# Issuing P's transpositions ahead of the output's product, and a group's sum of scales one stage after its squares

## The chip, the cores and the metric

The kernel runs on one core of one Trainium2 chip. A core has a matrix engine (TensorE, PE in the profile, with PEld for its loads of stationary operands), three engines for elementwise work (VectorE or DVE, ScalarE or ACT, GpSimd or POOL) and a sync engine (SyncE or SP), which here issues all transfers. Each engine takes its own list of instructions and waits on semaphores that the others raise. TensorE writes its results to PSUM, a small memory that VectorE and ScalarE read.

The metric is the device time of one execution in microseconds.

## The reference

Two batches of 512 tokens with 512 features go through one transformer layer in float32: causal attention with 32 query heads and 8 key and value heads of 128 features, the output product, a residual and a layer norm; then a feed-forward part, a residual and a layer norm.

```python
q = (hidden_states @ Wq)...; k = (hidden_states @ Wk)...; v = (hidden_states @ Wv)...
scores = einsum('bhqd,bhkd->bhqk', q, k) * HEAD_DIM ** -0.5     # causal
out = softmax(scores) @ v ; x = layernorm(x + out @ Wo)
base_out = x @ W_base.T + b_base
weights = sparsemax(x @ W_router.T + b_router)                  # 8 experts
expert_out = einsum(x @ lora_A, weights, lora_B)                # rank 16
x = layernorm(x + base_out + expert_out)
```

## The kernel before

**Groups, batches and steps.** A group is one key and value head with its four query heads. There are 8 groups and 2 batches, and each pair of a group and a batch is cut into 4 tiles of 128 query tokens. One such tile is a unit of work; the list `units` has 64 of them. The main loop runs over steps s = 0 to 59, and the last four units are worked off by `tail()`, which has an order written out by hand (`TAIL`). For most groups a batch's four steps are followed by the other batch's four, so a group takes eight steps. Within a pair, i = s mod 4 is the tile; this document calls its steps first, second, third and fourth. A causal tile i reads i + 1 blocks of keys, so later steps have more work.

**What a step issues.** The stages of a unit are spread over three steps:

- `unit_a` (this step's unit): four products of scores `s`, one for every 32 rows of the four heads together (L229, from the loop at L408); VectorE adds the mask and finds the maximum (L413), ScalarE takes the exponential with its row sums (L418); then `cut_p` writes P as a high and a low half in float16, the high half on ScalarE (L381), the low one on VectorE (L384), with the factors `ast` (L369, L371) between.
- `unit_t` (the previous step's unit): P, 6 to 30 blocks of 128 x 128 in the tile `phl`, is transposed by TensorE into PSUM tiles `px` (L340), eight blocks at a time, and ScalarE copies each eight to `pt` (L341). A copy of eight blocks is 1024 columns wide, the last of six is 768.
- `proj` (for the next pair): in the first step K and the first of Q's four products, in the second another of Q, in the third V, in the fourth the last two of Q. Each is 12 matmuls of 512 columns (V: 48 of 128), and its result is cut into halves by ScalarE and then VectorE (`cut_psum`, L233 and L234).
- `unit_c` (the unit of two steps ago): the output product `pw`, 12 matmuls of 512 columns, and a sum into `acc` on VectorE (L497).
- `unit_b` (the previous step's unit): P times V, `pv`, 6, 12, 18 or 24 matmuls, and its cut `o`.

The generator of `unit_t` is advanced by one group of eight blocks ahead of each projection, and what is left of it is issued later: before, right ahead of `unit_b` and after `unit_c`.

**PSUM buffers.** The tag `pj` has two buffers. The tiles `px`, the results of the projections (`pk`, `pq`, `pvp`), the sums `tot` and some of the feed-forward's tiles share them in turn. `S` has four (scores), `PV` and `wo` one each (`pv`, `pw`).

**Weights of a later group.** `prepare` loads a group's weights, finds their largest values (L123, VectorE), splits them into float16 halves on GpSimd (L117 to L120). Between stand the scales: `measure` takes the squares of the largest values on ScalarE (`sq`, L186), `total` adds them over the partitions with a product by ones on TensorE (`tot`, L128), and `scales` turns the sum into powers of two (L133 to L138, VectorE). This is done twice for a group: for Q, K and V in the four steps of a first batch, and for the output's rows in those of a second batch. `at(prepare(...), ...)` lists at which step each piece is issued, up to the generator's next `yield`; `advance` takes one piece after each projection and each `unit_b`, and the last call of a step takes all that are left.

**What sets the order.** The main loop's order in the source is a priority. The framework's scheduler places the instructions on each engine's list by this priority and by its own estimate of when operands and buffers are there. So the lists interleave the stages, and one moved line can move many instructions. The start (L777 on) and the tail are placed by hand.

Of the kernel before, what the change touches and what calls it, by code (L numbers as in the profile page):

```python
# [22 lines left out]
NG = 8  # L23
# [17 lines left out]
def kernel(  # L41
# [60 lines left out]
    def load_raw(src, name, rows=False):  # L102

        raw = sb.tile([P, 512], F32, tag="rawo" if rows else "raw", name=f"raw_{name}", bufs=4 if rows else 6)
        sync_load(raw, src if len(src.shape) == 2 else src.rearrange("p a c -> p (a c)"))
        return raw
# [6 lines left out]
    def split16(hi, lo, view, by, fast=False):  # L113

        if fast:
            first = nc.scalar.activation(hi, view, AF.Copy, scale=by)
        nc.gpsimd.tensor_scalar(view, view, by, 1.0, ALU.mult, ALU.mult)  # L117
        if not fast:
            first = nc.gpsimd.tensor_scalar(hi, view, 1.0, 1.0, ALU.mult, ALU.mult)
        return first.ins, nc.gpsimd.tensor_tensor(lo, view, hi, ALU.subtract).ins  # L120

    def amax(dst, view):
        nc.vector.tensor_reduce(dst, view, AX.X, ALU.max, apply_absolute_value=True)  # L123

    def total(sq, n, name, tag="pj"):

        tot = ps.tile([P, 8], F32, tag=tag, name=f"tot{name}", bufs=4 if tag == "S" else 2)
        nc.tensor.matmul(tot[:, :n], ones, sq[:, :n], start=True, stop=True)  # L128
        return tot

    def scales(sc, tot, n):

        nc.vector.tensor_scalar(  # L133
            tot[:, :n].bitcast(I32), tot[:, :n].bitcast(I32), 24, 23,
            ALU.logical_shift_right, ALU.logical_shift_left,
        )
        nc.vector.tensor_scalar(sc[:, 0, :n], tot[:, :n], 2.0**-109, 2.0 ** (64 - TOP), ALU.max, ALU.mult)
        nc.vector.reciprocal(sc[:, 1, :n], sc[:, 0, :n])  # L138
# [3 lines left out]
    def source(g, j):  # L142

        if j < 4:
            return wq[g * HPG + j]
        if j < 6:
            return (wk, wv)[j - 4][g]
        r0 = (g * HPG + j - 6) * P
        return wo[r0 : r0 + P, :]

    def w_tile(g, j):
        shape = [P, 2, KC, P] if j < 6 else [P, 2, HID]
        tag, bufs = ("w", 12) if j < 6 else ("wo", 8)
        W[(g, j)] = sb.tile(shape, F16, tag=tag, name=f"w{g}_{j}", bufs=bufs)
        return [W[(g, j)][:, q].rearrange("p a c -> p (a c)") if j < 6 else W[(g, j)][:, q] for q in range(2)]

    def prepare(g, js, raws=None):

        if raws is None:
            raws = [load_raw(source(g, j), f"{g}_{j}", j >= 6) for j in js]  # L160
            yield
        name = f"{g}_{js[0]}"
        rows = js[0] >= 6
        n = 1 if rows else 6
        if (g, rows) not in SC:
            yield from measure(g, js, raws, name, rows, n)
        sc = SC[(g, rows)]
        for k, (j, raw) in enumerate(zip(js, raws)):
            j = 0 if rows else j
            LAST[(g, js[k])] = split16(*w_tile(g, js[k]), raw, sc[:, 1, j : j + 1], g == 0)  # L170
            if k % 2:
                yield

    def measure(g, js, raws, name, rows, n):
        mx = sb.tile([P, 8], F32, tag="mx", name=f"mx{name}", bufs=2)
        for k, (j, raw) in enumerate(zip(js, raws)):
            j = k + 1 if rows else j
            with behind(mybir.EngineType.DVE) if g > 1 or rows else nullcontext():
                amax(mx[:, j : j + 1], raw)
            if k % 2:  # L180
                yield
        sc = sb.tile([P, 2, 8], F32, tag="sc", name=f"sc{name}", bufs=8)
        if rows:
            amax(mx[:, 0:1], mx[:, 1:5])
        sq = sb.tile([P, 8], F32, tag="sq", name=f"sq{name}", bufs=2)
        nc.scalar.activation(sq[:, :n], mx[:, :n], AF.Square)  # L186
        scales(sc, total(sq, n, name), n)
        SC[(g, rows)] = sc
        yield
# [153 lines left out]
    def proj(g, b, j):  # L343
        if j == 4:
            factors(g, b)
            end_k(g, b, mul_k(g, b))
        elif j == 5:
            end_v(g, b, mul_v(g, b))
            turn_v(g, b)
        else:  # L350
            end_q(g, b, j, mul_q(g, b, j))
# [79 lines left out]
    def unit_t(g, b, i, tag="pj"):  # L431

        phl = PH.pop((g, b, i))
        nb = 8 * i + 6
        PT[(g, b, i)] = pt = sb.tile([P, nb, P], F16, tag="PT", name=f"pt{g}_{b}_{i}", bufs=2)
        for k in range(0, nb, 8):
            n = min(nb, k + 8)
            turn_blocks(pt[:, k:n, :], phl[:, k * P : n * P], tag)
            yield
# [44 lines left out]
    def unit_c(g, b, i, first):  # L484
        o2 = OT.pop((g, b, i))
        if first:
            out_factor(g, b)
        pw = ps.tile([P, HID], F32, tag="wo", name=f"pw{g}_{b}_{i}", bufs=1)
        pairs = []
        for h in range(HPG):  # L490
            w2 = W[(g, 6 + h)]
            oh, ol = (o2[:, a, h].rearrange("p j q -> p (j q)") for a in range(2))
            pairs += [(oh, w2[:, 0, :]), (oh, w2[:, 1, :]), (ol, w2[:, 0, :])]
        mm3(pw, pairs)
        yield
        a = acc[b * NT + i]
        nc.vector.scalar_tensor_tensor(a, pw, LM[(g, b)][:, 7:8], a, ALU.mult, ALU.add)  # L497
        yield
# [94 lines left out]
    def behind(engine):  # L593

        return tc.issue_after(next(i for i in reversed(nc.cur_bb.bb.instructions) if i.engine == engine))
# [124 lines left out]
    def done(gen):  # L720
        for _ in gen:
            pass
# [3 lines left out]
    def step_ffn():  # L726
        for gen in list(live):
            if next(gen, "end") == "end":
                live.remove(gen)
# [7 lines left out]
    JS = (4, 0, 1, 5, 2, 3)  # L737
    ROWS = (6, 7, 8, 9)
# [38 lines left out]
    with tc.manual_schedule(engines={ET.PE, ET.DVE, ET.Activation, ET.Pool, ET.SP}):  # L777
# [10 lines left out]
        w1_raw = [load_raw(source(1, j), f"1_{j}") for j in JS[:2]]  # L788
# [81 lines left out]
    def step_live():  # L870
        step_ffn()
# [4 lines left out]
    def at(gen, *when):  # L876
        for u in when:
            plan[u].append(gen)
# [11 lines left out]
    def late_x(b, after):  # L890
        yield from behind_all(convert_x(b), *LAST[after])

    at(prepare(0, ROWS, wo_raw), 0, 0, 0)
    at(prepare(1, JS, w1_raw), 1, 1, 1, 2, 2, 2, 3, 3)
    at(prepare(1, ROWS), 4, 5, 5, 6, 6, 7, 7)
    at(late_x(1, (1, 3)), 5, 6, 7, 7)
    at(ffn_setup(), 20, 21, 21, 21, 21, 21, 28, 28, 29, 29, 36)
    for g in range(1, NG):
        u = NT * (starts[g] - 2) - (3 if g == NG - 2 else 0)
        if g > 1:  # L900
            at(prepare(g, JS), u - (1 if g == NG - 2 else 2), u, u, u + 1, u + 2, u + 2, u + 3, u + 3, u + 3)
        u += NT
        if g > 1:
            at(prepare(g, ROWS), u - 2, u, u + 1, u + 2, u + 2, u + 3, u + 3)

    def advance(last=False):
        while plan.get(s):
            next(plan[s].pop(0), None)
            if not last:
                break  # L910
# [44 lines left out]
    for s in range(len(units) - NT):  # L955
        if s < len(units):
            g, b, i = units[s]
            k = s // NT
            nx = groups[k + 1] if k + 1 < len(groups) else None
            done(unit_a(g, b, i))  # L960
            step_live()
            turns = unit_t(*units[s - LB]) if s >= LB else iter(())
            if nx:
                for j in ((4, 0), (1,), (5,), (2, 3))[i]:
                    next(turns, None)
                    proj(*nx, j)
                    advance()
            step_live()
        if s >= LC:
            n = s - LC  # L970
            u = units[n]
            done(unit_c(*u, n % NT == 0))
            step_live()
            if u[0] == NG - 1 and u[2] < NT - 1:
                live.append(ffn(u[2]))
        if s >= LB:
            done(turns)
            done(unit_b(*units[s - LB]))
            step_live()
            advance()  # L980
        advance(True)
# [58 lines left out]
```

## Time and profile before

| | us |
|---|---|
| Time, median of 3 (lowest, highest) | 780.69 (777.91, 781.45) |
| The profiled execution: its time | 780.98 |
| Its span in the profile | 779.2 |
| First, second, third, fourth step where nothing else falls in (s = 28, 29, 26, 27) | 11.70, 8.58, 8.55, 15.07 |
| Third and fourth step with the sum of an output group (s = 14, 15) | 9.46, 14.58 |
| ScalarE's copy of 1024 or 768 transposed columns, median of all | 1.00 |
| ScalarE's and VectorE's cut of a product of Q, median | 0.60, 0.69 |
| VectorE's sum of an output product into acc | 0.74 |

How it is read: a step's length is from the first scores product of one unit to that of the next. A row of the timeline gives the start, the length of the whole row, the engine, the line, the operation, the tiles written and read, and how many instructions it holds; in square brackets is the engine's idle time ahead of it and what ended it. The ends of matmuls are modelled and overlap the next start, so between rows of TensorE the difference of two starts tells more than start and end do. In the view of waits a row gives who waited for whom, the total, how often, and the longest.

### The profile page before, as it was taken

The page shows a single profiled execution, that of the slowest core. Times are in us where ns is not written, and L with a number is a line of the kernel's source. Part 1 is how long each engine was busy: PE and PEld are TensorE (multiplying, and loading weights), DVE is VectorE, ACT ScalarE, POOL GpSimd, SP SyncE. Part 2 cuts the span into 40 slices and gives each one's busy share as a digit, 9 for nine tenths or more (in the row PEclk, how much of TensorE's full clock was granted, in tenths as well). Part 3 has the DMA queues.
Part 4 walks back from the last instruction along what each step waited for, and adds up shares of the span by engine and source line. Part 5 has one row for each costly group of instructions (what it writes and reads, how often), then busy time and mean ns, then how long its engine had stood idle before and what let it go on. Part 6 is the DMA issues. An engine that isn't in the chain of part 4 may idle for free.

```text
span 779.2 us, 15455 instructions
## 1 busy us (share of the span) xinstructions
PE 739.1 (95%) x5630; PEld 465.6 (60%) x5630; DVE 528.4 (68%) x1701; ACT 512.2 (66%) x1294; POOL 314.3 (40%) x500
## 2 busy tenths in 40 slices
PE   9899999999998999999999999999999999998896
PEld 6666656555665755566565655666565656655653
DVE  6874866767584676748576675849576576865587
ACT  6797676767576676757577576757667676456630
POOL 5779350907036297633318067243615020200011
PEclk9899999999999999999999999999999999999999
DMA  8641110210102011110102012010000000000001
GB/s 314 213 136 41 43 55 2 55 28 29 28 2 69 2 42 56 28 55 1 55 3 82 1 55 82 2 55 1 1 1 2 2 1 1 15 14 14 1 7 64
DMA packets 17358, 32.22 MB, mean 41 GB/s; under 512 B 1920, under 2 KB 2176, under 8 KB 17280
## 3 DMA queue, kind: packets, MB, share of 16 engines
q1 hardware_dynamic: 17280, 31.22, 12.6%
q8 instruction: 44, 0.72, 0.4%
q14 instruction: 34, 0.28, 0.1%
HBM read 29.12 MB, written 2.10 MB: 40 GB/s over the span
## 4 chain that ended last, share of the span: by engine, by line
PE 35%; ACT 32%; DVE 18%; issue 5%; POOL 2%; DMA 0%; POOLq 0%; ACTq 0%; DVEq 0%
PE pq L229 11%; ACT s L418 10%; ACT pt L341 9%; ACT phl L381 8%; PE pw L229 7%; PE pv L229 7%; PE s L229 3%; DVE s L413 3%; PE px L340 3%; DVE mx L123 2%; ACT q L233 2%; DVE phl L384 2%; DVE q L234 2%; PE pa L229 2%; DVE o L234 1%
## 5 line engine op out<-in xcount | busy, mean ns | idle before, releaser
L229 PE MATMUL pw<-w,o 128*128 128x512 f16 x768 | 182.3, 380 | 0.0
L384 DVE SCALAR_TENSOR_TENSOR phl<-s,ast,phl 128x128 f16<-128x128 f32 (+7 forms) x352 | 128.7, 417 | 75.2 <-ACT phl L381 74.8
L341 ACT COPY pt<-px 128x1024 f16<-128x1024 f16 (+1 forms) x160 | 148.1, 937 | 44.0 <-PE px L340 43.6
L229 PE MATMUL pq<-xT,w 128*128 128x512 f16 x672 | 154.1, 379 | 7.6 <-DVE k L234 4.3
L413 DVE CUSTOM_DVE_ANT_0 s<-s,mask,lm 128x320 f32<-128x320 f32 (+15 forms) x256 | 118.9, 502 | 56.0 <-PE s L229 55.4
L418 ACT ACTIVATE s<-s,ast 128x320 f32<-128x320 f32 (+15 forms) x256 | 120.1, 471 | 33.8 <-DVE ast L413 30.0
L229 PEld LDWEIGHTS <-w 128*128 128x128 f16 x840 | 80.4, 98 | 100.8 <-issue 15.1
L381 ACT ACTIVATE phl<-s,ast 128x96 f16<-128x96 f32 (+11 forms) x304 | 122.3, 476 | 19.4 <-DVE ast L371 12.5
L229 PE MATMUL pv<-pt,vt 128*128 128x256 f16 (+1 forms) x960 | 113.8, 262 | 8.8 <-ACT pt L341 5.7
L229 PEld LDWEIGHTS <-o 128*128 128x128 f16 x768 | 73.6, 99 | 78.2 <-issue 1.4
L325 POOL TENSOR_SCALAR vt<-vt 64x512 f16<-64x512 f16 (+1 forms) x96 | 58.2, 611 | 144.5 <-ACT vt L233 121.0
L229 PE MATMUL s<-k,q 128*128 128x32 f16 (+15 forms) x768 | 109.3, 281 | 5.1 <-ACT pt L341 1.5
L229 PEld LDWEIGHTS <-vt 128*128 128x128 f16 x960 | 86.7, 98 | 28.8 <-issue 15.0
L340 PEld LDWEIGHTS <-phl 128*128 128x128 f16 x1152 | 76.7, 99 | 28.9 <-issue 4.5
L340 PE MATMUL px<-ident,phl 128*128 128x128 f16 x1152 | 90.3, 220 | 3.2 <-ACT pt L341 2.0
L234 DVE SCALAR_TENSOR_TENSOR q<-pq,q 128x512 f16<-128x512 f32 x56 | 38.7, 691 | 63.6 <-ACT q L233 62.1
L229 PEld LDWEIGHTS <-q 128*128 128x128 f16 x768 | 63.2, 99 | 28.1 <-issue 5.2
L120 POOL TENSOR_TENSOR w<-raw,w 128x512 f16<-128x512 f32 x70 | 79.9, 1164 | 0.2
L233 ACT ACTIVATE o<-pv 128x512 f16<-128x512 f32 x64 | 38.6, 602 | 59.4 <-PE pv L229 56.2
L233 ACT ACTIVATE q<-pq 128x512 f16<-128x512 f32 x56 | 34.5, 616 | 60.1 <-PE pq L229 60.1
L261 POOL TENSOR_SCALAR lm<-sc,xs 128x1 f32<-128x1 f32 x15 | 4.1, 271 | 152.9 <-DVE acc L497 130.9
L418 ACT ACTIVATION_READ_ACCUMULATOR s<-s,ast 128x1 f32 x256 | 54.0, 211 | 0.0
(175 smaller groups left out, 860.4 us busy)
## 6 DMA issues: line engine op xcount, KB each, us to landing
raw<-in_wo_dram SPq DMA_DIRECT2D x32, 256.0 KB, 2.8
raw<-in_wq_dram SPq DMA_DIRECT2D x29, 256.0 KB, 2.9
xraw<-in_xt_dram SPq DMA_DIRECT2D x8, 256.0 KB, 5.1
raw<-in_wk_dram SPq DMA_DIRECT2D x8, 256.0 KB, 2.7
raw_x<-in_xt_dram SPq DMA_DIRECT2D x8, 256.0 KB, 4.3
acc<-in_x_dram SPq DMA_DIRECT2D x8, 256.0 KB, 6.1
out_dram<-y SPq DMA_DIRECT2D x8, 256.0 KB, 2.0
raw<-in_wv_dram SPq DMA_DIRECT2D x7, 256.0 KB, 2.9
```

The source lines that it names most:

```text
L120: return first.ins, nc.gpsimd.tensor_tensor(lo, view, hi, ALU.subtract).ins
L123: nc.vector.tensor_reduce(dst, view, AX.X, ALU.max, apply_absolute_value=True)
L229: nc.tensor.matmul(dst, a, b, start=first and j == 0, stop=last and j == n - 1)
L233: nc.scalar.activation(hi, psrc, AF.Copy, scale=by)
L234: return nc.vector.scalar_tensor_tensor(lo, psrc, by, hi, ALU.mult, ALU.subtract).ins
L325: nc.gpsimd.tensor_scalar(dst, src, 1.0, 1.0, ALU.mult, ALU.mult)
L340: nc.tensor.transpose(px[:, k, :], src[:, k * P : (k + 1) * P], ident16)
L341: nc.scalar.copy(dst, px[:, :n, :])
L381: nc.scalar.activation(dst, src, AF.Copy, scale=by)
L384: nc.vector.scalar_tensor_tensor(dst, src[:, at : at + k], by, p[:, at : at + k], ALU.mult, ALU.subtract)
L413: nc.vector.tensor_tensor_reduce(out=sc[:, :n], in0=sc[:, :n], in1=mask[:, S - n :], scale=lm[:, 0:1], scalar=BIG, op0=ALU.add, op1=ALU.mi ...
L418: nc.scalar.activation(sc[:, :n], sc[:, :n], AF.Exp, bias=st[:, 0, j : j + 1], scale=-1.0, accum_out=st[:, 1, j : j + 1])
```

## The change

The rest of `unit_t`'s generator is issued right after the projections and ahead of `unit_c`. In `measure` a `yield` stands between the squares and the sum, and each list of steps for `prepare` has one more entry, so that the squares are issued one stage earlier and the sum where it was.

```diff
         sq = sb.tile([P, 8], F32, tag="sq", name=f"sq{name}", bufs=2)
         nc.scalar.activation(sq[:, :n], mx[:, :n], AF.Square)
+        yield
         scales(sc, total(sq, n, name), n)
...
-    at(prepare(1, JS, w1_raw), 1, 1, 1, 2, 2, 2, 3, 3)
-    at(prepare(1, ROWS), 4, 5, 5, 6, 6, 7, 7)
+    at(prepare(1, JS, w1_raw), 1, 1, 1, 1, 2, 2, 2, 3, 3)
+    at(prepare(1, ROWS), 4, 5, 5, 5, 6, 6, 7, 7)
...
-            at(prepare(g, JS), u - (1 if g == NG - 2 else 2), u, u, u + 1, u + 2, u + 2, u + 3, u + 3, u + 3)
+            at(prepare(g, JS), u - (1 if g == NG - 2 else 2), u, u, u + 1, u + 1, u + 2, u + 2, u + 3, u + 3, u + 3)
...
-            at(prepare(g, ROWS), u - 2, u, u + 1, u + 2, u + 2, u + 3, u + 3)
+            at(prepare(g, ROWS), u - 2, u, u + 1, u + 1, u + 2, u + 2, u + 3, u + 3)
...
             step_live()
+        done(turns)
         if s >= LC:
...
         if s >= LB:
-            done(turns)
             done(unit_b(*units[s - LB]))
```

The start and the tail are the same in both.

## The prediction

> **What bounds the kernel now.** I read the page's busy shares first, then TensorE's waits, then the timeline of single steps, because a matrix engine at 95% leaves few microseconds and only a timeline shows which wait ends last.
>
> ```profile
> span 779.2 us, 15455 instructions
> PE 739.1 (95%) x5630; PEld 465.6 (60%) x5630; DVE 528.4 (68%) x1701; ACT 512.2 (66%) x1294; POOL 314.3 (40%) x500
> ```
>
> TensorE sets the time, the other engines have a third of theirs free. Busy counts modelled ends, so I measure TensorE by the starts of successive rows. In the first-step window below 6 output products start over 1.29 us (0.215 each) and 14 transpositions over 0.78 us (0.056 each): where it doesn't wait, nothing is lost between instructions. So a time changes only by what TensorE waits, and by chains that hold it.
>
> ```profile
> PE pv L229 <- ACT pt L341: 5.7, 8, 2.2
> PE tot L128 <- ACT sq L186: 4.4, 7, 0.8
> PE pq L229 <- DVE k L234: 4.3, 11, 0.5
> ```
>
> The view of waits counts only gaps above 0.15 us after a modelled end. By starts the same waits are larger, and those on P's copy are many more than eight. Step s is one tile of one batch; i = s mod 4 (0 to 3) makes it first, second, third or fourth. First step, s = 28/29:
>
> ```profile
> 342.85 1.46 PE L229 MATMUL pw<-w,o 128*128 128x512 f16 x6
> 343.05 0.60 ACT L233 ACTIVATE q<-pq 128x512 f16<-128x512 f32 x1 [2.66 <-PE pq L229]
> 343.68 0.69 DVE L234 SCALAR_TENSOR_TENSOR q<-pq,q 128x512 f16<-128x512 f32 x1 [3.47 <-ACT q L233]
> 344.14 0.94 PE L340 MATMUL px<-ident,phl 128*128 128x128 f16 x14
> 344.79 1.71 ACT L341 COPY pt<-px 128x1024 f16<-128x1024 f16 x2 [1.15 <-PE px L340]
> 344.92 1.42 PE L229 MATMUL pv<-pt,vt 128*128 128x256 f16 x13
> 346.18 0.23 PE L229 MATMUL s<-k,q 128*128 128x160 f16 x1
> 346.55 1.36 PE L229 MATMUL pv<-pt,vt 128*128 128x256 f16 x11
> ```
>
> Two copies of P run on ScalarE in one go (1.71), and the 14th product with V waits for the second: from 346.18 to 346.55 TensorE has 0.07 us of work (one scores product), so 0.30 us of waiting. It recurs in 13 first steps (0.26 to 0.30). Fourth step, s = 27:
>
> ```profile
> 332.12 0.50 PE L340 MATMUL px<-ident,phl 128*128 128x128 f16 x6
> 332.45 2.19 PE L229 MATMUL pv<-pt,vt 128*128 128x256 f16 x18
> 332.65 0.80 ACT L341 COPY pt<-px 128x768 f16<-128x768 f16 x1 [0.38 <-PE px L340]
> 333.51 0.86 PEld L229 LDWEIGHTS <-vt 128*128 128x128 f16 x8 [0.19 <-issue]
> ```
>
> 18 products with V are 1.80 us of work (15 of 256 columns at 0.109, 3 of 128 at 0.056); the next row starts 2.03 us on: 0.23 us of waiting, in nine fourth steps. Third step, first with the sum of an output group (s = 14), then with that of Q, K, V (s = 26):
>
> ```profile
> 179.53 1.46 PE L229 MATMUL pw<-w,o 128*128 128x512 f16 x6
> 181.51 0.23 ACT L186 ACTIVATE sq<-mx 128x1 f32<-128x1 f32 x1
> 181.79 0.38 PE L128 MATMUL tot<-sq,ones 128*128 128x1 f32 x2 [0.80 <-ACT sq L186]
> ```
>
> ```profile
> 318.58 0.49 PE L340 MATMUL px<-ident,phl 128*128 128x128 f16 x6
> 318.68 1.03 ACT L381 ACTIVATE phl<-s,ast 128x352 f16<-128x352 f32 x2 [0.88 <-DVE tot L133]
> 319.60 0.80 ACT L341 COPY pt<-px 128x768 f16<-128x768 f16 x1
> 320.45 0.81 PE L229 MATMUL pv<-pt,vt 128*128 128x256 f16 x6 [0.53 <-ACT pt L341]
> ```
>
> In the first, ScalarE reaches the squares late and TensorE stands 0.97 us (181.79 less 179.53 and 6 x 0.215). In the second the copy at 319.60 stands behind ScalarE's softmax work, not behind the transpositions; TensorE waits 0.69 us.
>
> **The change part by part.** No instruction is added or removed on any engine; SP's order of transfers is the same. The order of the built program tells what moves.
>
> (a) First steps. Before: six output products, 14 transpositions, 13 products with V, wait. After: eight transpositions, five output products, six transpositions, one output product, 24 products with V. From the rows: Q's product ends at 342.85; eight transpositions (0.45) to 343.30, their copy follows Q's cut on ScalarE, 343.55 to 344.55; five output products (1.08) to 344.38. The last six need the PSUM buffer of Q's product, free when VectorE's cut ends at 343.68 + 0.69 = 344.37: a new wait of about 0.05. They end at 344.77, their copy runs 344.96 to 345.76. One output product and 13 products with V take TensorE to 346.25, 0.5 us after the copy. So 0.30 goes and 0.05 comes: 13 x 0.25 = 3.25 us.
>
> (b) Fourth steps. Three output products (0.65) now stand between the last six transpositions and the products with V. The transpositions start at 331.47; ScalarE does Q's cut first (to 332.27), then the copy, 332.2 to 333.0; the tenth product with V comes at 333.27. The 0.23 is gone where nothing else holds ScalarE: eight steps (s = 11, 15, 23, 27, 35, 47, 51, 59), 1.8 us. Not s = 19, where the copy stands behind ScalarE's wait for a transfer of the FFN's setup (2.01 us at 241.13).
>
> (c) The squares a stage earlier. They stand ahead of the third step's exponentials, and the sum directly behind V's product. Summed over seven steps the waits for them are 5.5 us by starts (0.38 to 0.97). Most is not won, since the chain of the second fence comes next: third and fourth step take 9.46 + 14.58 = 24.04 us at s = 14 and 50, and 8.55 + 15.07 = 23.62 without such a wait (s = 10, 18, 26, 34): 0.42 each, 0.84. At s = 22 the pair is 23.60 already: 0. At s = 38/39 0.85 goes, and 0.45 comes back, because the next Q's product has six output products ahead instead of nine: 0.40. At s = 6 and 30 the last six transpositions come two output products behind the sum and wait for VectorE's reading of it: at s = 30 it could be read at 361.0, TensorE is there at 360.23, so 0.97 is paid there instead of the 0.95 for the squares: 0. Their fourth steps fall in with the regular ones: waits of 0.77 and 1.07 become 0.35: 0.42 + 0.72. At s = 43 0.38 and 0.23 become about 0.26: 0.35. Together 2.7.
>
> (d) Third steps without a sum (s = 42, 54) transpose directly behind V's product, twelve output products ahead of the products with V: waits of 1.05 and 0.51 go, 1.5.
>
> (e) Third steps with the sum of Q, K, V (four): the copy is held by ScalarE, so TensorE stops at the same moment; but all three matmuls of the first scores product now precede the stop, 0.1 each, 0.4.
>
> (f) Steps 46, 55 to 58: 0 + 0.3 - 0.4 (at 58 the transpositions wait for VectorE's row at 679.49, 0.68 long, about 0.5 us behind them).
>
> Covers. The squares cost nothing on ScalarE: 0.23 us ahead of work that waits for scores anyway; uncovered, 0.2 x 14 = 2.8 us. In second steps P's copy moves ahead of the second to fourth exponential on ScalarE; by the rows at 348 that makes them about 1.2 us later, and P's last low part still ends (about 354.7) before its row of before (355.62), since the high parts are no longer split by Q's cut. That cut moves behind them and ends about 355.4 on VectorE; V's product, which takes its buffer, starts at 356.92. GpSimd swaps V's copies (6 x 0.61) with a weight's split (5 us) at two places; the products that read V come 35 us later (94.74 against 130). Output sums on VectorE (0.74) wait for later products, and behind them stands only the next step's first maximum, which waits for later scores too. The tail's order is unchanged; its waits follow its own chain: 0, between -2 and +2, the spread of what one stall there costs (1.38 at 711).
>
> The Trainium skill, TensorE: Matmul & The Clock Gate, Part 2 (step-by-step), says that weight loads are pulled ahead but matmuls stay in program order. That speaks against the change: a transposition that waits for its buffer holds the output products behind it. Were products able to pass, (a) would be 13 x 0.30 = 3.9. The rows agree with the page: no product starts inside the waits above.
>
> Sum: 3.25 + 1.8 + 2.7 + 1.5 + 0.4 - 0.1 = 9.6 us. The profiled execution took 780.98 (span 779.2), 0.3 above the median of 780.69: 780.98 - 9.6 = **771.4 us**.
>
> **Rivals.** *ScalarE sets the moment anyway.* Copies of P end when ScalarE's queue lets them, so (a) and (b) return as waits one row later, as in (e). For it: 66% busy and the second fence above. Against it: in (a) ScalarE idles 1.15 us before its copies, in (b) 0.38. Gain 4.5: 776.4.
>
> *The buffer comes late: slower.* The moved transpositions wait in front of the output products for a PSUM buffer. In first steps the margin is nil (344.37 against 344.38). If ScalarE takes P's copy ahead of Q's cut, or the cut runs that much later, the six stand 0.9 us (one copy's row): 13 x 0.65 paid instead of 3.25 won is +11.7, so 783; and if at s = 6, 30, 46 and 58 they wait for V's cut instead of the sum's reading (364.26 against 361.2 at s = 30), up to 3 each more, 795. I take 788. It decides from about 0.6 us of lateness in each of 17 places. Against it: the built program has Q's cut first, and waits on the sum's reading at 6, 30 and 46.
>
> *More than counted.* Copies done earlier also shorten the waits of Q's products (0.54 in first, 0.35 in fourth steps), which hang on ScalarE's queue; a third of them over 26 steps is 4 us: 767.4. Against it: these chains start at the step's scores, which don't move.
>
> **How the numbers follow.** The measurement tells 0.5% (3.9 us) from no change: 776.8 and 784.6 are the bounds. As worked out 0.63 (its own range 768 to 775: the tail's +-2 and the terms (c), (f)); ScalarE 0.20, half of it within 0.5%; buffer late 0.09; more 0.08. Faster 0.81, same 0.10, slower 0.09. The range leaves out the late buffer and the outer half of the richest case: 766.5 to 779.5.
>
> **What would show it.** Right: first steps have six transpositions between output products and no gap ahead of the 14th product with V (11.45 instead of 11.70 us a step); in the view of waits tot <- ACT sq is gone and pv <- ACT pt shrinks, with its longest (2.2, the transfer) left; pq <- DVE k stays near 4.3. Wrong: px waiting for DVE q or DVE vt with 0.5 us or more a time, or pq waiting longer than before.

## The result, and the profile after

The changed kernel takes 768.12 us (median of 4, 767.37 to 771.40) against 780.57 before: a ratio of 0.986 [0.984, 0.989]. Measured once more it takes 768.81 against 779.29, 0.987 [0.984, 0.990]. The forecast was 771.4 with a range of 766.5 to 779.5. The profiled execution took 768.57 where that of before took 780.98: 12.4 us less, where 9.6 were forecast.

The span and the busy times on the page of the changed kernel:

```profile
span 766.8 us, 15482 instructions
...
PE 731.3 (95%) x5630; PEld 462.0 (60%) x5630; DVE 531.4 (69%) x1701; ACT 509.9 (66%) x1294; POOL 313.9 (41%) x500
```

TensorE is busy 7.8 us less with the same 5630 matmuls, so the modelled busy time holds a part of what was won, and a part of what a slower clock cost (below). TensorE's waits (who waited for whom, line numbers one higher than before; total, times, longest):

```profile
PE pq L230 <- DVE k L235: 4.5, 12, 0.4
PE pv L230 <- ACT pt L342: 2.8, 3, 2.4
PE pq L230 <- DVE q L235: 2.4, 6, 1.2
...
PE px L341 <- DVE ast L372: 1.4, 5, 0.5
...
PE px L341 <- DVE vt L235: 0.5, 2, 0.2
```

The sum of scales no longer waits for the squares (4.4 us before, no line now). Products with V that wait for P's copy went from 5.7 us in 8 places to 2.8 in 3, and one of these is the transfer's 2.4. The first product of Q waits for K's cut as it did (4.3, now 4.5). The two lines of `px` are new: transpositions that wait in third steps. One sign of being wrong did come, in small: products of Q wait longer than before, by starts 13.7 us in steps 4 to 59 instead of 11.7 (the wait for Q's cut was 0.6 in the view before). It comes mainly at s = 43 (0.62), at 55 and 56 (0.5 more each), and at step 20 (0.53), where before has none.

A first step, s = 28/29, in the timeline:

```profile
337.11 0.61 PE L341 MATMUL px<-ident,phl 128*128 128x128 f16 x8
...
337.56 1.24 PE L230 MATMUL pw<-w,o 128*128 128x512 f16 x5
...
337.94 0.69 DVE L235 SCALAR_TENSOR_TENSOR q<-pq,q 128x512 f16<-128x512 f32 x1 [3.47 <-ACT q L234]
...
338.69 0.49 PE L341 MATMUL px<-ident,phl 128*128 128x128 f16 x6
...
339.22 0.80 ACT L342 COPY pt<-px 128x768 f16<-128x768 f16 x1 [0.40 <-PE px L341]
339.23 2.62 PE L230 MATMUL pv<-pt,vt 128*128 128x256 f16 x24
...
341.69 0.91 PE L230 MATMUL s<-k,q 128*128 128x160 f16 x9
```

The six transpositions stand between the output products, and 24 products with V follow without a stop: from 339.23 to 341.69 are 2.46 us for 24 products of which 21 have 256 columns (21 x 0.109 + 3 x 0.056 = 2.46). The forecast had one new wait of 0.05, and it is here: five output products from 337.56 end at 338.64, VectorE's cut ends at 338.63, the transpositions start at 338.69. The step itself is not the 11.45 us that were forecast but 12.94, because the next step's first scores product now follows all 24 products with V, where before it followed 13. The second step is shorter by more than that, 7.08 instead of 8.58: the two together take 20.02 instead of 20.28, so the forecast 0.25 is there.

A third step with the sum of Q, K, V, s = 26:

```profile
312.47 0.69 DVE L235 SCALAR_TENSOR_TENSOR vt<-pvp,vt 128x512 f16<-128x512 f32 x1 [0.17 <-ACT vt L234]
...
313.14 0.17 DVE L133 TENSOR_SCALAR tot<-tot 128x6 int32<-128x6 int32 x1
313.21 0.50 PE L341 MATMUL px<-ident,phl 128*128 128x128 f16 x6 [0.23 <-DVE ast L372]
...
313.31 1.02 ACT L382 ACTIVATE phl<-s,ast 128x352 f16<-128x352 f32 x2 [0.88 <-DVE tot L133]
...
314.23 0.80 ACT L342 COPY pt<-px 128x768 f16<-128x768 f16 x1
...
315.08 0.82 PE L230 MATMUL pv<-pt,vt 128*128 128x256 f16 x6
```

Here the stop is only cut in two. The transpositions wait 0.40 for V's cut (ends 313.16), and the copy at 314.23 still stands behind ScalarE's softmax work, so the products with V wait another 0.30 in the middle: 0.69 before, and 0.10 in front of the transpositions, against 0.70 now.

**What of the 12.4 us is the change's.** The starts of the same scores products, compared in both traces, give 0.89 us ahead of step 4, 9.89 from there to the scores of the second of the last four units, where the table's last window ends too, and 1.67 behind. The table sets the middle part against the forecast; a window runs from the scores of one third step to those of the next, so that products that changed places with scores fall inside one window. The forecast is the sum of the prediction's terms that lie in it.

| Steps | Forecast | Measured |
|---|---|---|
| 4-5 | 0.25 | 0.25 |
| 6-9 | 0.67 | 0.97 |
| 10-13 | 0.58 | 0.52 |
| 14-17 | 0.90 | 0.94 |
| 18-21 | 0.35 | 1.28 |
| 22-25 | 0.48 | 0.60 |
| 26-29 | 0.58 | 0.54 |
| 30-33 | 0.97 | 1.50 |
| 34-37 | 0.58 | 0.25 |
| 38-41 | 0.65 | 1.06 |
| 42-45 | 1.65 | 1.19 |
| 46-49 | 0.48 | 0.15 |
| 50-53 | 0.90 | 0.94 |
| 54-59 | 0.64 | -0.30 |
| Sum | 9.7 | 9.9 |

Part of it is the clock: the profile says what share of its full clock TensorE was granted. Windows of the trace of before (busy time of PE, PEld, DVE, ACT and POOL, then the granted clock, then transfers):

```profile
24.00:66.00 42.00, 38.68 (x241) 27.51 (x242) 30.73 (x102) 37.04 (x94) 33.36 (x49) 0.92 0.45 145
...
243.00:247.00 4.00, 3.17 (x29) 2.77 (x29) 1.91 (x8) 2.33 (x10) 2.74 (x7) 0.65 0.41 131
...
715.00:719.00 4.00, 3.77 (x17) 2.06 (x17) 2.18 (x9) 3.10 (x9) 0.00 (x0) 0.57 0.00 0
```

and of the same places in the changed kernel:

```profile
24.00:65.00 41.00, 37.30 (x241) 26.27 (x241) 31.11 (x103) 37.07 (x96) 31.04 (x46) 0.96 0.45 144
...
239.00:243.00 4.00, 2.67 (x33) 2.17 (x33) 2.66 (x11) 2.91 (x13) 3.21 (x7) 1.00 0.41 125
...
704.00:708.00 4.00, 3.55 (x24) 1.93 (x24) 2.41 (x9) 3.01 (x9) 0.00 (x0) 1.00 0.01 2
```

In the execution of before that was profiled TensorE ran slower at the start (0.92 against 0.96), at 0.65 behind the long wait of step 19, and at 0.57 in the tail. At the last place four output products lie 0.43 us apart instead of 0.215, among others, and this is the 1.67. Behind the wait of step 19 five products with V cost 0.105 too much each, and step 20, whose first rows are slow too, takes 12.23 us where other first steps of before take 11.70: together about 1.05. The kernel with only the fourth steps moved, granted the full clock there, gains 1.03 in steps 18 to 21, though its forecast there is nothing. On TensorE's list nothing is moved before 74 us or behind 699 us, and 0.87 of the 0.89 arose before step 1, where no engine's list differs. So the change itself is worth about 9.89 - 1.05 = 8.8 us, and the forecast of 9.6 was close.

The repeated executions agree. In the second measurement, four executions of before at a clock of 0.999 took 775.7 to 776.5 us and five at 0.990 to 0.992 took 780.4 to 781.4; the changed kernel took 768.3 at 0.998 and 768.7 and 769.7 at 0.993 and 0.994, where before took 778.8 and 779.3 at 0.994. At like clocks the gain is between 7.4 and 10.6 us.

### The profile page after: what moved, and what is told of

Its sections match the earlier page's. It is cut to its first block, busy times and chain, and to the rows that moved or that the text cites. A ratio compares the mean times of both kernels' runs of the same rounds, so it can differ in the third digit from the quotient of the medians.

```text
span 766.8 us, 15482 instructions
## 1 busy us (share of the span) xinstructions
PE 731.3 (95%) x5630; PEld 462.0 (60%) x5630; DVE 531.4 (69%) x1701; ACT 509.9 (66%) x1294; POOL 313.9 (41%) x500
## 4 chain that ended last, share of the span: by engine, by line
PE 45%; ACT 25%; DVE 15%; issue 5%; POOL 2%; DMA 0%; POOLq 0%; ACTq 0%; DVEq 0%
PE pq L230 13%; PE pv L230 10%; PE pw L230 8%; ACT s L419 8%; ACT phl L382 7%; PE s L230 5%; ACT pt L342 5%; PE px L341 4%; PE pvp L230 2%; DVE phl L385 2%; DVE mx L123 2%; DVE s L414 2%; ACT o L234 2%; DVE q L235 2%; PE pa L230 1%
## 5 line engine op out<-in xcount | busy, mean ns | idle before, releaser
L230 PE MATMUL pw<-w,o 128*128 128x512 f16 x768 | 185.6, 379 | 0.0
L342 ACT COPY pt<-px 128x1024 f16<-128x1024 f16 (+1 forms) x160 | 149.8, 938 | 31.1 <-PE px L341 30.9
L382 ACT ACTIVATE phl<-s,ast 128x96 f16<-128x96 f32 (+11 forms) x304 | 121.2, 482 | 17.6 <-DVE ast L372 10.9
L230 PE MATMUL pv<-pt,vt 128*128 128x256 f16 (+1 forms) x960 | 107.9, 262 | 3.7 <-ACT pt L342 2.8
L230 PE MATMUL s<-k,q 128*128 128x480 f16 (+15 forms) x768 | 103.5, 279 | 5.1 <-ACT pt L342 1.5
L117 POOL TENSOR_SCALAR raw<-raw,sc 128x512 f32<-128x512 f32 x70 | 47.7, 691 | 19.2 <-issue 13.4
```

What stands on the lines that cost most here:

```text
L230: nc.tensor.matmul(dst, a, b, start=first and j == 0, stop=last and j == n - 1)
L342: nc.scalar.copy(dst, px[:, :n, :])
L382: nc.scalar.activation(dst, src, AF.Copy, scale=by)
```

## The experiments

All times are medians, and each is set against runs of the kernel before on the same chip.

**Only the transpositions.** Before, with `done(turns)` ahead of `unit_c`, and `measure` as it was.

```diff
+        done(turns)
         if s >= LC:
...
         if s >= LB:
-            done(turns)
             done(unit_b(*units[s - LB]))
```

> Only the transpositions are moved; the squares stay where they were. Theory of the prediction (each part pays for itself): first steps give 13 x 0.30 = 3.9 us, fourth steps 8 x 0.23 less 0.05 each = 1.4, third steps without a sum 1.5, the sums' waits (tot for ACT sq, 4.4 in the view of waits) stay: 6 to 8 us faster than before, ratio 0.990 to 0.992. Rival 'ScalarE sets the moment': without the squares' move the copies of P in third and fourth steps end when they did, so 3 us or less, ratio 0.996 or more. Rival 'the surplus of the changed kernel (12.4 us measured, 9.6 forecast) is made by the transpositions': 10 us, ratio 0.987.

773.69 against 779.11: 5.4 us, ratio 0.9939 [0.9922, 0.9955]. That is less than worked out (the interval ends just short of 0.992), and more than "ScalarE sets the moment" gives. The trace shows one place that costs it: at s = 43 the planner (the framework's scheduler) put eight transpositions ahead of the fourth product of Q, which then waits 1.70 us for their copy; steps 42 to 45 lose 0.78 where the full change wins 1.19. In the changed kernel the same product waits 0.62. Why the planner chose that order is open: here the sum of scales waits 0.88 us for its squares just before, but the kernel with only the first steps moved (below) has the same 1.70 without such a wait.

**Only the squares.** The changed kernel with `done(turns)` back behind `unit_c`; the `yield` and the lists stay.

```diff
-        done(turns)
         if s >= LC:
...
         if s >= LB:
+            done(turns)
             done(unit_b(*units[s - LB]))
```

> Only the squares are moved a stage ahead; the transpositions stay. Theory of the prediction: 2.7 us faster, a little less without the other part, 1.5 to 3 us, ratio 0.996 to 0.998; tot waiting for ACT sq is gone from the view of waits, and pv waiting for ACT pt grows by about half of it. Rival 'all of the sums' waits comes back one row later': ratio 1.000. Rival 'all 5.5 us of the waits are won': ratio 0.993.

774.34 against 779.11: 4.8 us, ratio 0.9947 [0.9930, 0.9964], more than expected. In its trace only 3.6 us lie between step 4 and step 60; the start is 0.8 earlier, as in the others. By places: s = 14 and 50 give 0.30 and 0.38 (forecast 0.42 each), s = 22 0.13 (0), s = 38/39 0.45 (0.40), s = 43 0.34 (0.35), but s = 6/7 and 30/31 give 0.96 and 0.97 where the prediction had 0.42 and 0.72. So the miss is there. As expected, about half of the removed 4.4 us came back one row later: products with V that wait for P's copy rose from 5.7 to 7.8 us.

**Only first steps, only fourth steps.** Before, with the move tied to the step:

```diff
+        if s % NT == 0:          # the other kernel: == 3
+            done(turns)
         if s >= LC:
```

> The transpositions are moved in first steps alone, nothing else. Theory of the prediction: the wait of 0.30 us ahead of the 14th product with V goes in 13 steps, 3.3 to 3.9 us, ratio 0.995 to 0.996; first and second step together get shorter by 0.25 to 0.30. Rival 'given back in the next step, where P's copy now stands ahead of the exponentials': first and second step together keep their 20.28 us, ratio 0.999 to 1.000. Rival 'the buffer comes late': px waits for Q's cut, ratio above 1.000.

> The transpositions are moved in fourth steps alone, nothing else. Theory of the prediction: the wait of 0.23 us ahead of products with V goes in eight steps: 1.8 us, ratio 0.9975, and up to 0.5 less if the next Q's product waits 0.05 longer each time, as it does in the changed kernel. Rival 'ScalarE sets the moment': ratio 1.000. Rival 'the rest of the surplus lies here': 4 us, ratio 0.995.

First steps: 774.75, 4.4 us, 0.9952 [0.9933, 0.9970]. Fourth steps: 777.25, 1.9 us, 0.9983 [0.9969, 0.9997]. Both lie where the prediction's terms (3.25 and 1.8) put them. In the traces a first and second step together get 0.25 to 0.27 us shorter in nine of thirteen places, so nothing is given back when P's copy stands ahead of the second step's exponentials; a third and fourth step together get 0.24 or 0.25 shorter in seven of the eight places. With first steps alone other windows moved beyond the term, by -1.0 at steps 42 to 45 and by +0.7 at steps 30 to 33 among others, where the planner placed other rows otherwise too; that the total fits is in part luck. Both traces have the tail's 1.67 and a start that is 1.07 and 2.68 us earlier at step 4, at clocks of 0.996 and 0.998: in the second of them nothing is changed before step 3. The kernel with only the squares moved had a slow stretch in the tail again (0.57 for 4 us), and there its tail is only 0.19 shorter. That is why these two amounts aren't counted for the change.

**The changed kernel again.**

> The changed kernel once more, beside the kernel before on the same chip. The two profiled executions differ by 12.4 us, of which 0.9 arose before step 4 and 1.7 behind step 60, where nothing is changed; the profiles with one part alone have the same 0.8 to 2.7 at the start and mostly the same 1.7 at the end, so they are put down to the execution of before that was profiled. Theory: the change is worth the 9.9 us between step 4 and step 60, ratio 0.987 to 0.988, and 9.5 us is what the two parts alone came to (5.3 and 4.2). Rival 'the change reaches the start and the tail too': 12.4 us, ratio 0.984.

768.81 against 779.29: 10.5 us, ratio 0.9868 [0.9839, 0.9896]. The interval holds both values, so it is the clocks above that decide for the smaller. The two parts alone, 5.4 and 4.8, add to 10.2.

**The sum of scales in another buffer.** In third steps the stop in front of the transpositions has to do with who gets the two `pj` buffers. `PV` is idle from the cut of the previous unit's result up to this step's products with V.

```diff
-    def total(sq, n, name, tag="pj"):
+    def total(sq, n, name, tag="PV"):
```

> The changed kernel, with the sum of scales written to the PSUM buffer of the products with V instead of one of the two that the transpositions use. In the changed kernel the last six transpositions of a third step with a sum wait 0.18 to 0.40 us for a buffer, 11 times, and the products with V behind them 0.17 to 0.30. Theory 'the buffer makes the wait': both go, 3 to 6 us faster than the changed kernel, ratio to before 0.980 to 0.984. Rival 'ScalarE sets the moment': the first wait comes back as a longer one of the products with V, 1 us or less, ratio 0.986 to 0.988.

765.98, 2.8 us less than the changed kernel; ratio to before 0.9829 [0.9799, 0.9859]. The gain is at the lower end of "the buffer makes the wait" (in the traces 3.2 us from step 4 to step 60), and the 0.986 of the rival lies just outside the interval. The waits between output products and transpositions fell from 6.0 to 1.7 us by starts. The third step of above, s = 26:

```profile
308.61 0.49 PE L341 MATMUL px<-ident,phl 128*128 128x128 f16 x6
308.94 2.75 PE L230 MATMUL pw<-w,o 128*128 128x512 f16 x12
...
310.47 0.83 ACT L342 COPY pt<-px 128x768 f16<-128x768 f16 x1
...
311.49 1.03 ACT L382 ACTIVATE phl<-s,ast 128x352 f16<-128x352 f32 x2
...
311.73 1.31 PE L230 MATMUL pv<-pt,vt 128*128 128x256 f16 x12
```

The transpositions no longer wait for V's cut, their copy runs ahead of ScalarE's high parts of P (L382) instead of behind them, and the twelve products with V follow each other. Of the 0.70 us of waiting 0.20 are left, in front of the first of these products. So in the changed kernel it was the buffer that put the copy behind ScalarE's softmax work. A part of the gain came back at other places:

```profile
PE pq L230 <- DVE q L235: 4.9, 13, 1.2
...
PE pv L230 <- ACT pt L342: 3.4, 2, 2.9
```

Products of Q now wait 4.9 us for Q's cut instead of 2.4, though only 1.0 more over all their waits (14.8 against 13.8 by starts), and the one wait behind the transfer grew from 2.4 to 2.9.

**Two products of Q in another buffer.** Of what is left in the changed kernel the largest recurring wait is that of the first and fourth product of Q, 28 times 13.8 us by starts.

```diff
-            end_q(g, b, j, mul_q(g, b, j))
+            end_q(g, b, j, mul_q(g, b, j, "PV" if j in (0, 3) else "pj"))
```

> The changed kernel, with the first and the fourth product of Q written to the PSUM buffer of the products with V. In the changed kernel the first product of Q waits 0.53 us for K's cut to free a buffer in 13 first steps, the fourth 0.40 for the third's cut in 11 fourth steps. Theory 'the buffer makes the wait': 8 to 11 us faster than the changed kernel, ratio to before 0.973 to 0.978. Rival 'ScalarE sets the moment': the transpositions behind them wait for the copies of P instead, half or less, ratio 0.981 or more.

749.20, 19.6 us less than the changed kernel; ratio to before 0.9620 [0.9588, 0.9651]. The same first step:

```profile
321.51 0.61 PE L341 MATMUL px<-ident,phl 128*128 128x128 f16 x8
...
321.96 2.75 PE L230 MATMUL pq<-xT,w 128*128 128x512 f16 x12
...
324.55 0.94 PE L341 MATMUL px<-ident,phl 128*128 128x128 f16 x14
...
325.33 2.75 PE L230 MATMUL pw<-w,o 128*128 128x512 f16 x12
...
327.92 2.62 PE L230 MATMUL pv<-pt,vt 128*128 128x256 f16 x24
```

The product of Q follows the second eight transpositions at once, and the whole output product comes behind the last transpositions, where it covers their copy. No row stands still: each of these differences is the work itself (12 x 0.216 = 2.59, 14 x 0.056 = 0.78). A first step is 0.58 shorter and a fourth 0.40, as expected; the surplus is 3.0 us before step 5, 1.9 at steps 55 and 56, and 2.9 at step 19. There the copy of the last six blocks stood behind ScalarE's wait for a transfer:

```profile
236.00 0.50 PE L341 MATMUL px<-ident,phl 128*128 128x128 f16 x6
...
237.63 0.63 ACT L521 ACTIVATE warm<-raw_lorab 128x512 bf16<-128x512 f32 x1 [2.14 <-DMA raw_lorab<-in_lora_b_dram]
...
239.49 0.79 ACT L342 COPY pt<-px 128x768 f16<-128x768 f16 x1
...
240.33 1.14 PE L230 MATMUL pv<-pt,vt 128*128 128x256 f16 x9 [2.36 <-ACT pt L342]
```

With the product of Q early the same transpositions come ahead of that wait, and the copy with them; the transfer now holds nothing that TensorE needs:

```profile
227.77 0.50 PE L341 MATMUL px<-ident,phl 128*128 128x128 f16 x6
...
229.50 0.88 ACT L342 COPY pt<-px 128x768 f16<-128x768 f16 x1
...
230.69 1.97 PE L230 MATMUL pv<-pt,vt 128*128 128x256 f16 x18
...
231.89 0.63 ACT L521 ACTIVATE warm<-raw_lorab 128x512 bf16<-128x512 f32 x1 [0.94 <-DMA raw_lorab<-in_lora_b_dram]
```

The Trainium skill, Perfetto Trace Analysis, Optimization Strategy, says that the same gap repeating on the engine that should be saturated can mean too few buffers for the next tile. The trace agrees: 28 gaps of 0.49 us on average, gone when two tiles take a buffer that is idle at that time.

**A later cut of Q.** VectorE's cut of the first product of Q is done twice, so that its buffer comes free 0.69 us later.

```diff
+        for _ in range(times - 1):       # times: 2 for the first product of Q, else 1
+            nc.vector.scalar_tensor_tensor(lo, psrc, by, hi, ALU.mult, ALU.subtract)
         return nc.vector.scalar_tensor_tensor(lo, psrc, by, hi, ALU.mult, ALU.subtract).ins
```

> The changed kernel, with VectorE's cut of the first product of Q in each pair done twice, so that the PSUM buffer that the last six transpositions of a first step take comes free 0.69 us later. TensorE's order is kept in all first steps. Theory of the prediction ('a late buffer holds the output product and all behind it'): the margin was nil, so 0.6 to 0.7 us in 13 steps, 8 to 9 us slower than the changed kernel, ratio to before 0.998 to 0.999, with px waiting for DVE q, some 0.65 a time. Rival 'there is slack': TensorE comes to the transpositions later than the buffer by half a microsecond or more, and 0 to 3 us are lost, ratio 0.991 or less.

773.68, 4.9 us more than the changed kernel; ratio to before 0.9929 [0.9901, 0.9956]: neither, by the median. In the trace a first step loses 0.19, steps 4 to 60 together 2.8, which is within the rival's 0 to 3, though not for its reason. The rest is in the tail, which has a slow stretch here (0.78 and 0.79 in two windows of 4 us), and at the start, where the order differs too. The reason for the 0.19:

```profile
339.39 1.24 PE L230 MATMUL pw<-w,o 128*128 128x512 f16 x5
339.64 1.01 ACT L344 COPY pt<-px 128x1024 f16<-128x1024 f16 x1
...
340.50 0.69 DVE L237 SCALAR_TENSOR_TENSOR q<-pq,q 128x512 f16<-128x512 f32 x1
340.69 0.49 PE L343 MATMUL px<-ident,phl 128*128 128x128 f16 x6
```

The transpositions start at 340.69, in the middle of the second cut (to 341.19), so they don't wait for it: they have the other buffer, that of the third eight transpositions, whose copy ends at 340.65. The reading is that the planner, which gives out buffers when the program is built, had the longer cut in its estimate of when each comes free; no run shows its estimate, but in this step TensorE's order is the same in both kernels. The copy's end is 0.22 behind the last of the five output products (339.39 + 1.08 = 340.47), where the changed kernel had 0.05. So a lateness that the planner knows was capped by the other buffer here. What a lateness would cost that it doesn't know was not tried.

**Both in the other buffer, and the products of Q without the change.** The first kernel has the edits of the two buffer experiments together, on top of the change. The second has that of Q alone, on the kernel before.

> The changed kernel with the sum of scales and the first and fourth product of Q all written to the PSUM buffer of the products with V. The sum alone gave 2.8 us over the changed kernel, the products of Q alone 19.6. Theory 'the two add': 746.4 us, ratio to before 0.957 to 0.959. Rival 'what the sum's move gave back (the products of Q waited 1.3 us more, from 13.8 to 15.1) can't be given back here': 4.3 us more than the products of Q alone, 745, ratio 0.955 to 0.957. Rival 'one buffer for all of them becomes the wait': 749 us or more.

> The kernel before, with the first and the fourth product of Q written to the PSUM buffer of the products with V; neither part of the change. Theory 'the parts are independent': the move of Q's products gives here what it gave the changed kernel, 19 us, so 760 us, ratio 0.974 to 0.978, and the change on top of it is worth its 10 us (749.2 against 760). Rival 'the change makes room for it': products of Q that start earlier wait for the copies of P, 8 to 14 us, ratio 0.982 to 0.990, and the change on top is worth more than 15.

Both: 746.97 against 778.42, ratio 0.9599 [0.9578, 0.9620]. This beats both kernels of this case, by 31 and 21 us. It is nearest to what adding the two gains gives (746.4); the rival's ratio of 0.955 to 0.957 lies outside the interval, while the 749 of the third, 0.961 to 0.962, lies at its upper end. The traces decide for adding: from step 4 to step 60 the sum's move gives 3.2 us here and gave 3.2 in the changed kernel. On the kernel before: 763.68 against 778.42, 14.7 us, ratio 0.9817 [0.9792, 0.9843], between the two expectations, with an interval that reaches into the second. So the change is worth 763.7 - 749.2 = 14.5 us there (measured on two chips; 13.4 in the traces from step 4 to step 60), more than by itself. The traces show where part of the surplus lies: step 19 keeps its wait of 2.34 us with the products of Q alone, and loses it only when the transpositions come early too, 2.7 us between the two.

## Why the prediction was right

**(a) First steps: right.** Forecast 0.25 a time, and 0.25 to 0.27 came, with the 0.05 of new waiting in its place. Weak was only the reason given for the risk. The prediction feared 0.6 us of lateness at a buffer with no margin; the margin is nil, but when the cut was made longer the planner handed out the other buffer.

**(b) Fourth steps: right.** 0.23 forecast, 0.24 alone, and in the changed kernel the fourth product of Q waits 0.05 longer.

**(c) Squares and sums: too small at two places.** The step that failed is "it could be read at 361.0, TensorE is there at 360.23, so 0.97 is paid there" for s = 30 (and 6). The moment of VectorE's reading was taken from rows of before, behind VectorE's softmax factors. In the changed kernel:

```profile
353.61 0.33 PE L128 MATMUL tot<-sq,ones 128*128 128x1 f32 x2
...
353.98 0.17 DVE L133 TENSOR_SCALAR tot<-tot 128x1 int32<-128x1 int32 x1 [0.20 <-PE tot L128]
...
354.45 0.14 DVE L137 TENSOR_SCALAR sc<-tot 128x1 f32<-128x1 f32 x1
...
354.64 0.49 PE L341 MATMUL px<-ident,phl 128*128 128x128 f16 x6 [0.24 <-DVE sc L137]
```

The sum comes directly behind V's product, as forecast, and VectorE reads it in a gap ahead of its last factors, at 353.98, which is 359.97 on before's scale (the start of this step is 5.99 earlier). TensorE waits 0.40 for its last reading instead of the 0.95 that it paid for the squares. The two windows gave 2.47 where 1.64 was forecast. The other five places of (c) came within 0.15 us each when the squares were moved alone.

**(d) Third steps without a sum: the waits went, their worth did not all arrive.** Waits of 1.05 and 0.51 are gone at s = 42 and 54, but the windows are 0.46 and 0.94 short. At s = 55 the chain is plain:

```profile
617.54 2.51 PE L230 MATMUL s<-k,q 128*128 128x416 f16 x12
...
618.42 0.69 DVE L601 BATCH_NORM_STATS2 lna<-acc 128x6 f32<-128x512 f32 x1
...
619.25 0.63 DVE L414 CUSTOM_DVE_ANT_0 s<-s,mask,lm 128x416 f32<-128x416 f32 x1
...
626.67 2.75 PE L230 MATMUL pq<-xT,w 128*128 128x512 f16 x12 [1.19 <-DVE q L235]
```

VectorE's first maximum comes 1.71 us after the first scores, behind the layer norm's statistics; 11 us later in before it stood at 630.28, 2.31 after the scores at 627.97. It moved by 11.03 and so by no more than all earlier gains (11.09 at the scores of s = 54), so the half microsecond won at s = 54 is waited out at the fourth product of Q (1.35 by starts, 0.80 before). At step 56 the first product of Q waits 0.67, 0.16 before. This is the rival "ScalarE sets the moment" in one place, with VectorE at the head of the chain. For s = 42 the rows of the step behind it wait 0.16, 0.62 (the fourth product of Q) and 0.17, where before had 0.38 and 0.23 and the forecast 0.26.

**(e) Third steps with the sum of Q, K, V: too large, 0.4 for about 0.1, and for the wrong reason.** The stop stayed nearly as long (0.10 + 0.69 against 0.40 + 0.30), and at s = 34 it became longer (0.69 + 0.30). The prediction had it that "the copy is held by ScalarE". The kernel with the sum in the other buffer shows that in the changed kernel the transpositions were held first, by a buffer: without that the copy runs ahead of the same softmax work, and 0.70 becomes 0.20.

**(f) Steps 46 and 58: worse than forecast.** At s = 46 new waits of 0.28 (transpositions behind ScalarE's high part of P) and 0.18 came where 0 was forecast, and at s = 58 the transpositions wait 0.82 instead of about 0.5.

**The total** missed by 2.6 to 3.3 us (768.1 and 768.8), mostly because the sum was set against an execution with a clock of 0.990. That 9.6 is so near to 8.8 in the same steps is in part luck: 0.8 too little at two places of (c) hides a part of what (d), (e) and (f) lack.

**The rivals.** "ScalarE sets the moment" is refuted for first and fourth steps by the two kernels with these alone, and in third steps with the sum of Q, K, V ScalarE holds the copy only because the transpositions come late. "The buffer comes late" shows as the 0.16 to 0.69 in front of the transpositions of third steps, and the kernel with the sum in the other buffer prices it at 2.8 us in all. "More than counted" would have shortened the waits of Q's products; they kept their 0.53 and 0.40, and the kernel with these products elsewhere shows why: they waited for a buffer, not for ScalarE's queue.

## What to carry to other kernels

Count a recurring wait by the starts of instructions, step by step; the waits of first and fourth steps were under a third of a microsecond each, and half of the forecast came from them. Where the same short wait recurs in front of a matmul, ask first which buffer its result goes to, and whether another one is idle at that time: this gave 19.6 us on top of the reordering and 14.7 without it, where the reordering gave about 10. When a gain is summed against one execution, look at the granted clock of that execution first, since here the spread of the same kernel (775.7 to 781.4 us) was over half of the gain.

## What was not expected of the hardware

After a wait of 2.40 us at step 19 TensorE's granted clock was 0.65 for 4 us in one execution, and after a like wait of 2.52 us it was 1.00 in another; in the tail 0.57 and 1.00 with the same instructions. The Trainium skill, TensorE: Matmul & The Clock Gate, Part 1 (the HAM clock gate), says that the clock is set by windows of activity that run freely and don't start with the kernel, so that the number of slow products at a kernel's start varies from run to run. These traces agree with that as far as they go: a like gap was followed by a slow stretch or by none. In the slow stretches TensorE's rows take twice their usual distance (output products 0.43 for 0.216 us, transpositions 0.106 for 0.056), for about 3.4 us each: 244.3 to 247.7 and 715.3 to 718.7 in the trace of before. Fewer and shorter waits seem to go with a steadier clock (the executions of the kernel with Q's products in the other buffer have 0.996 to 0.999, those of before 0.990 to 0.999), but no run here tests that by itself.
